# End of a routing stage: scatters one per step, four buffers for places, and the tile table made per partition, ahead of a branch

## The chip, the cores and the metric

The kernel runs on one core of one Trainium2 chip. The metric is the device time of one execution in microseconds (us); below 1% of it, about 22 us, two kernels can hardly be told apart by a few runs, since the runs shown of one kernel differ by as much. PE is TensorE, DVE VectorE, ACT ScalarE, POOL GpSimd and SP SyncE, which here only issues transfers.

## The reference

Two sublayers on 4096 nodes of width 512, with 8 attention heads of 64, 8 experts of 512 hidden units, and 2 experts chosen per node:

```python
x = x + gnn(layernorm(x), adj)          # attention over the neighbours in adj
x = x + moe(layernorm(x))

def moe(xf):
    logits = xf @ Wg + bg                        # 8 experts
    topk_scores, topk_idx = top_k(logits, 2)
    topk_w = softmax(topk_scores)
    h = gelu(einsum('nd,edh->neh', xf, W1) + b1)
    y = einsum('neh,ehf->nef', h, W2) + b2
    sel = take_along_axis(y, topk_idx[:, :, None], axis=1)
    return sum(topk_w[:, :, None] * sel, axis=1)
```

The adjacency matrix is sparse: the attention works on lists of neighbours. In the second sublayer only the two chosen experts of each node are worked out, on tiles of rows that belong to one expert.

## The kernel before

There are three stages.

1. **Projections and lists**: keys, values and queries of all nodes go to DRAM, and lists of neighbours are made.
2. **Attention**: 32 tiles of 128 nodes. For each tile a loop runs over items, one for the diagonal and one for each 128 listed neighbours (L1177 and following). An item's keys, values and mask are fetched nine items ahead (AHEAD = 9) by `fetch`, mostly with indirect transfers issued by POOL. The order of all instructions in this loop is written out by hand (`manual_schedule`), with a step per item.
3. **Feed-forward** (`work_off`): 69 tiles (MOSTLY = NB - 2, NB = 71), each with 128 rows of one expert, read from a DRAM buffer `xs_d` that is ordered by expert.

Between 2 and 3 lies **routing**. When an attention tile is done, its rest runs in the steps after it, as numbered pieces (`piece`), and a group of tiles (four at a time, and for the last tiles 2, 1 and 1) is then routed by a list of `jobs`, one per step in which no other piece uses PE. `route_1` ranks the experts of each node and adds to `count`, the number of nodes per expert and partition. `route_2` and `route_3` find each node's two places in `xs_d` (`slot_i`, whole numbers, L808 and L809) and its two weights. `route_4` issues one scatter on POOL: 128 rows of 2064 bytes to their places. Scatters wait in the list `waiting`. `fetch` issues one in every third step (L263). In the last nine steps nothing is fetched, and the scatters that are left go out either when piece 6 of a later group finds them (then with `at_once`, which lets each wait for the one before to have landed), or in the loop that ends the stage:

```python
while waiting and waiting[0][0] < g - 1:
    waiting.pop(0)[1](True)
```

After the last step, SP loads W2 (eight transfers of 1 MB, L1215) into room that the attention's tiles leave. Then a test of the softmax sums (`bad`, `least`, `redo`, L1227 to L1237) decides whether a slow exact path has to be run: every engine loads `redo` into a register (L1241) and branches (`tc.If(again > 0)`, L1244). With the given inputs the exact path is skipped. In the skipped path each engine brings the semaphores to where the other path would leave them, and SP waits there for its transfers.

Only then comes `finish_routing` (L836 to L893): one product with a matrix of ones sums `count` over the partitions (`pn`). DVE works out, for all 71 tiles of the feed-forward side by side in the free dimension, in every partition alike, which expert a tile belongs to and at which row of `xs_d` it begins. Operations that compare tiles with experts have 71 x 8 = 568 elements per partition. The results are `table` (experts and first rows as whole numbers in one partition), `first` (each partition's row in each tile), `mine` (whether the row belongs to this tile) and `beyond` (whether a 70th and 71st tile exist).

In `work_off`, `fetch(b)` has SP load the tile's first row and expert from `table` into registers (L1372, L1368), then issue the read of 128 rows (L1377) and of two biases (L1379, L1380). PE transposes the rows (`transposed`, L209), multiplies by W1 (L1391), transposes again (L1403), multiplies by W2 (L1420), and POOL adds the weighted rows to the output (L1434).

Outside the attention loop the order of instructions on an engine is a scheduler's, from their order in the program and their dependencies. Inside an engine they are worked off in that order.

Of the kernel before, what the change touches and what calls it, by code (L numbers as in the profile page):

```python
# [43 lines left out]
def kernel(  # L44
# [747 lines left out]
    def route_3(m, l, rank, pp, rows, pool, name):  # L792
# [15 lines left out]
        slot_i = pool.tile([P, m, 2], I32, tag="slot_i", name=f"slot_i_{name}")  # L808
# [27 lines left out]
    def finish_routing(pool, psum):  # L836

        pn = psum.tile([P, E], F32, name="pn")
        nc.tensor.matmul(pn, ones, count, start=True, stop=True)
        many = pool.tile([P, E], F32, name="many")  # L840
        nc.vector.tensor_copy(many, pn)
        more = pool.tile([P, E, NT], F32, name="more")
        nc.vector.tensor_tensor(
            more, many.unsqueeze(2).to_broadcast([P, E, NT]),
            full.unsqueeze(1).to_broadcast([P, E, NT]), op=ALU.is_gt,
        )
        tiles_e = pool.tile([P, E], F32, name="tiles_e")
        nc.vector.tensor_reduce(tiles_e, more, axis=AX.X, op=ALU.add)
        none = pool.tile([P, E], F32, name="none")
        nc.vector.memset(none, 0.0)  # L850
        upto = pool.tile([P, E], F32, name="upto_e")
        nc.vector.tensor_tensor_scan(
            upto, tiles_e, none, initial=0.0, op0=ALU.add, op1=ALU.add
        )
        nc.vector.tensor_scalar(
            none[:1, :1], upto[:1, E - 1 : E], -float(MOSTLY), 0.0, op0=ALU.add, op1=ALU.max
        )
        nc.vector.tensor_copy(beyond, none[:1, :1])
        past = pool.tile([P, NB, E], F32, name="past_e")
        nc.vector.tensor_tensor(  # L860
            past, nth.unsqueeze(2).to_broadcast([P, NB, E]),
            upto.unsqueeze(1).to_broadcast([P, NB, E]), op=ALU.is_ge,
        )

        end = pool.tile([P, E + 1], F32, name="end")
        nc.vector.memset(end[:, E:], float(E * R + P))
        nc.vector.tensor_add(end[:, :E], many, start_e)
        more_e = pool.tile([P, E], F32, name="more_e")
        nc.vector.tensor_sub(more_e, end[:, 1:], end[:, :E])
        ends = pool.tile([P, NB, E], F32, name="ends")  # L870
        nc.vector.tensor_mul(ends, past, more_e.unsqueeze(1).to_broadcast([P, NB, E]))  # L871
        till = pool.tile([P, NB], F32, name="till")
        nc.vector.tensor_reduce(till, ends, axis=AX.X, op=ALU.add)
        expert = pool.tile([P, NB], F32, name="expert")
        nc.vector.tensor_reduce(expert, past, axis=AX.X, op=ALU.add)
        nc.vector.tensor_mul(past, past, tiles_e.unsqueeze(1).to_broadcast([P, NB, E]))  # L876
        nc.vector.tensor_reduce(first, past, axis=AX.X, op=ALU.add)  # L877
        nc.vector.tensor_sub(first, nth, first)
        nc.vector.tensor_scalar(first, first, float(P), float(P), op0=ALU.mult, op1=ALU.add)
        nc.vector.scalar_tensor_tensor(  # L880
            first, expert, float(R), first, op0=ALU.mult, op1=ALU.add
        )
        nc.vector.tensor_scalar_min(first, first, float(E * R))
        nc.vector.tensor_scalar_min(expert, expert, float(E - 1))

        nc.vector.tensor_scalar(till, till, end[:, 0:1], -float(P), op0=ALU.add, op1=ALU.add)
        begin = pool.tile([P, NB], F32, name="begin")
        nc.vector.tensor_tensor(begin, first, till, op=ALU.min)
        nc.vector.tensor_copy(table[:, :NB], expert[:1])
        nc.vector.tensor_copy(table[:, NB:], begin[:1])  # L890
        nc.vector.tensor_add(begin, begin, number.to_broadcast([P, NB]))
        nc.vector.tensor_tensor(mine, begin, first, op=ALU.is_ge)
        nc.vector.tensor_copy(first, begin)  # L893
# [8 lines left out]
    with tc.tile_pool(name="p2a", bufs=2) as two, tc.tile_pool(  # L902
# [15 lines left out]

        half_q = fixed.tile([P, 2, Q4], F32, name="half_q")
# [257 lines left out]
        for n, (i, c) in enumerate(items):  # L1177
            begin()
            if n + AHEAD < len(items):
                fetch(n + AHEAD)  # L1180
            if c == 2 and i + 1 < NT:
                load_q(i + 1)
# [16 lines left out]
            if c == listed[i] - 1:  # L1199
# [11 lines left out]
        nth = endp.tile([P, NB], F32, name="nth")  # L1211
        nc.gpsimd.iota(nth, pattern=[[1, NB]], base=0, channel_multiplier=0,
                       allow_small_or_imprecise_dtypes=True)
        for e in range(E):
            nc.sync.dma_start(out=w2[:, e], in_=W2[e].rearrange("(c p) f -> p c f", p=P))  # L1215
        order.__exit__(None, None, None)
        n = len(items)
        while n <= len(items) + LAST or jobs or first_of_step:
            begin()
            later(n)  # L1220
            while waiting:
# [3 lines left out]

        bad = small.tile([P, NT, 5], F32, name="bad")
        nc.vector.tensor_single_scalar(bad[:, :, 0], fine[:, :, 0], HIGH, op=ALU.is_lt)  # L1227
        nc.vector.tensor_single_scalar(bad[:, :, 1], fine[:, :, 1], 1.0 / LOW, op=ALU.is_lt)
        nc.vector.tensor_single_scalar(
            bad[:, :, 2:].rearrange("p i k -> p k i"), longer, 0.5, op=ALU.is_lt  # L1230
        )
        least = small.tile([P, 1], F32, name="least")
# [272 lines left out]
```

## Time and profile before

| | |
|---|---|
| time, median of 4 runs | 2244.66 us (2228.38 to 2251.49) |
| profiled execution | 2248.23 us, span 2246.5 us |
| mean granted TensorE clock | 0.964 |
| busy, share of the span | PE 93%, DVE 57%, POOL 45%, ACT 41% |
| feed-forward, first PE instruction | 1696.28 us |
| DMA while W2 is loaded (1655 to 1684 us) | 392 GB/s |

The profile is of one execution. Times in it are microseconds from the span's start, durations of single instructions partly in ns. "A <- B" names what an instruction waited for, and "issue" is time in which no wait was seen. PEclk is the TensorE clock that was granted, as a share of the full one; DMA share is the mean busy share of the 16 DMA engines, which comes out a little over 1 when all are full. A row with a "q" (SPq, DVEq) is of an engine's queue of instructions, where branches, waits and register work stand that don't count as busy.

### The profile page before, as it was taken

How to read it: one execution, taken by the hardware profiler on the slowest of the kernel's cores; microseconds unless marked ns; L12 is line 12 of the kernel's file. 1: busy time of each engine (PE TensorE's matmuls, PEld its weight loads, DVE VectorE, ACT ScalarE, POOL GpSimd, SP SyncE). 2: the span in 40 equal slices, each digit the busy share in tenths (PEclk: the TensorE clock that was granted, in tenths of full speed). 3: DMA queues.
4: the chain of work that ended last, by engine and by line, in shares of the span. 5: the costliest groups of instructions: out<-in, count | busy, mean ns of one | idle time of the engine just before them, and what ended most of it. 6: DMA issues, size and time to landing. Idle time of an engine off the chain costs nothing. (4 is left out here: it accounts for less than half of the span.)

```text
span 2246.5 us, 48528 instructions
## 1 busy us (share of the span) xinstructions
PE 2083.8 (93%) x18748; PEld 1384.3 (62%) x18748; DVE 1288.8 (57%) x2446; ACT 931.7 (41%) x1703; POOL 1020.0 (45%) x1067
## 2 busy tenths in 40 slices
PE   8978999899999999989999999998957999999998
PEld 3434444577778777777777777776743444444444
DVE  5786685376666656756666666665663333333332
ACT  3544444354555445545445454454531222222222
POOL 1044455476665565565565555566631111221121
PEclk9999999899999999999999999998988999999999
DMA  8977997677777677777787877766665666566664
GB/s 330 364 269 280 294 317 232 193 227 212 222 242 228 212 234 235 226 226 230 229 244 232 238 220 225 218 200 207 200 246 124 137 139 133 133 133 136 142 136 85
DMA packets 213087, 479.03 MB, mean 213 GB/s; under 512 B 48962, under 2 KB 80962, under 8 KB 208756
## 3 DMA queue, kind: packets, MB, share of 16 engines
q0 software_dynamic: 78944, 241.65, 36.8%
q1 hardware_dynamic: 133380, 233.15, 34.3%
q8 instruction: 153, 2.51, 0.5%
q10 hardware_dynamic: 528, 1.05, 0.1%
q14 instruction: 82, 0.67, 0.1%
HBM read 398.85 MB, written 76.90 MB: 212 GB/s over the span
## 5 line engine op out<-in xcount | busy, mean ns | idle before, releaser
L231 POOL DMA_INDIRECT kv<-kv_d,key_of x363 | 404.9, 1115 | 399.8 <-PE po L1024 239.7
L1012 DVE TENSOR_TENSOR e<-e,mask 128x512 f32<-128x512 f32 (+1 forms) x363 | 322.5, 889 | 304.8 <-ACT e L1004 148.2
L957 ACT COPY kT<-pk 128x512 f32<-128x512 f32 x395 | 232.3, 588 | 368.8 <-PE pk L954 215.6
L1024 PE MATMUL po<-e,kv 128*64 128x64 f32 (+1 forms) x5808 | 323.5, 250 | 16.7 <-issue 16.4
L1030 DVE TENSOR_TENSOR acc<-acc,e 128x512 f32<-128x512 f32 (+1 forms) x363 | 321.1, 885 | 2.8 <-PE po L1024 1.7
L1434 POOL DMA_INDIRECT out_dram<-y,to x69 | 107.7, 1561 | 453.0 <-ACT y L1426 442.0
L231 POOL DMA_INDIRECT mask<-in_adjT_dram,mask_of x234 | 277.8, 1187 | 72.8 <-issue 63.4
L1024 PEld LDWEIGHTS po<-e,kv 128*64 128x64 f32 x5808 | 252.3, 139 | 68.7 <-issue 24.6
L1001 PE MATMUL s<-q,kT 128*128 128x128 f32 x1832 | 281.2, 299 | 0.2
L1391 PE MATMUL ph<-w,xT 128*128 x552 | 251.7, 599 | 1.0 <-ACT xT L210 1.0
L1420 PE MATMUL py<-w,hT 128*128 x552 | 248.6, 593 | 1.5 <-DVE hT L1405 1.5
L1001 PEld LDWEIGHTS s<-q,kT 128*128 128x128 f32 x1832 | 236.0, 201 | 17.4 <-issue 1.2
L954 PE MATMUL pk<-ident,kv 64*128 64x64 f32 x2904 | 178.2, 241 | 49.8 <-issue 28.3
L954 PEld LDWEIGHTS pk<-ident,kv 64*128 64x128 f32 x2904 | 124.7, 143 | 121.3 <-issue 82.2
L1004 ACT ACTIVATE e<-s 128x512 f32<-128x512 f32 x229 | 137.7, 601 | 94.9 <-PE s L1001 54.3
L994 ACT ACTIVATE e<-s 128x512 f32<-128x512 f32 x268 | 147.3, 597 | 65.7 <-PE po L1024 26.2
L989 PE MATMUL s<-q,kT 64*128 64x128 f32 x2144 | 161.2, 282 | 3.6 <-issue 2.5
L1391 PEld LDWEIGHTS ph<-w,xT 128*128 128x128 f32 x552 | 100.5, 192 | 101.8 <-issue 100.2
L1420 PEld LDWEIGHTS py<-w,hT 128*128 128x128 f32 x552 | 99.6, 190 | 102.2 <-issue 99.5
L231 POOL DMA_INDIRECT pm<-in_adjT_dram,mask_of x129 | 126.1, 977 | 74.8 <-issue 30.8
L1426 ACT ACTIVATE y<-y,gate 128x512 f32<-128x512 f32 x69 | 49.8, 722 | 256.9 <-DVE y L1425 252.5
L1429 DVE SCALAR_TENSOR_TENSOR to<-r,spare,mine 128x1 f32<-128x1 int32 x69 | 15.2, 220 | 232.5 <-DMA r<-xs_d 232.5
(611 smaller groups left out, 2742.8 us busy)
## 6 DMA issues: line engine op xcount, KB each, us to landing
adjT<-in_adjT_dram SPq DMA_DIRECT2D x32, 2048.0 KB
bb<-in_L_ffn_b_dram SPq DMA_DIRECT2D x138, 256.0 KB
r<-xs_d SPq DMA_DIRECT2D x69, 258.0 KB
kv_d<-kv SPq DMA_DIRECT2D x32, 512.0 KB
xt<-in_x_dram SPq DMA_DIRECT2D x32, 256.0 KB
qT_d<-qT SPq DMA_DIRECT2D x8, 1024.0 KB
q<-qT_d SPq DMA_DIRECT2D x64, 128.0 KB
xr<-in_x_dram SPq DMA_DIRECT2D x32, 256.0 KB
```

What stands on the lines that cost most here:

```text
L231: nc.gpsimd.indirect_dma_start(out=to, out_offset=None, in_=src, in_offset=bass.IndirectOffsetOnAxis(ap=of[:, at[i] + c : at[i] + c + 1], ...
L954: nc.tensor.transpose(pk[:, r, ts(p, KD)], kv[n][half, ts(p, P)], ident[half, half])
L957: nc.scalar.copy(kT[n].rearrange("k p (r j) -> k r p j", r=2), pk[:, :, : NP * KD].rearrange("k r (p j) -> k r p j", p=NP),)
L989: nc.tensor.matmul(s[r][:, p, :], k[rows, p, :], q_in[i][rows, p, r, :], start=True, stop=True,)
L994: nc.scalar.activation(e.rearrange("p (a r) q -> p r a q", r=2)[:, r], s[r], AF.Exp)
L1001: nc.tensor.matmul(s[:, p], k[:, p, :], q_in[i][:, p, :, q], start=True, stop=True)
L1004: nc.scalar.activation(e, s.rearrange("p a r q -> p (a r) q"), AF.Exp)
L1012: nc.vector.tensor_mul(e, e, m.unsqueeze(1).to_broadcast(e.shape))
L1024: nc.tensor.matmul(po[i][r * KD : (r + 1) * KD, p, q], v[:, ts(h, KD)], e[:, h, :], start=(c < 0 and p == 0), stop=(c == listed[i] - 1), s ...
L1030: nc.vector.tensor_add(acc[i][:, :, q], acc[i][:, :, q], e)
L1391: nc.tensor.matmul(ph, xTs[b][:, c, :], w1[:, bass.ds(es[b], 1), c, :], start=(c == 0), stop=(c == DC - 1),)
L1420: nc.tensor.matmul(py, hTs[b][:, c, :], w2[:, bass.ds(es[b], 1), c, :], start=(c == 0), stop=(c == HC - 1),)
```

## The change

Four parts:

- In the last nine steps of the attention loop, where nothing is fetched, each step issues one scatter if any waits, behind a memset of one column on POOL.
- `slot_i` has four buffers instead of the pool's two.
- The test of the softmax sums is put among the last steps of routing (`check_all` at the fourth step after the last item) instead of behind them.
- `finish_routing` is called ahead of the branch, and once more inside it, at the end of the exact path. It works out one tile per partition: tile number = partition number, experts in the free dimension (8 elements per operation), then spreads expert, first row and a third column over all partitions by a diagonal matrix of 3 x 71 columns and a product with a matrix of ones. The number of tiles of an expert comes from a shift instead of a comparison with 32 multiples.

```diff
-        slot_i = pool.tile([P, m, 2], I32, tag="slot_i", name=f"slot_i_{name}")
+        slot_i = pool.tile([P, m, 2], I32, tag="slot_i", bufs=4, name=f"slot_i_{name}")
...
-    def finish_routing(pool, psum):
+    def finish_routing(all_ones, pool, psum, tag, name):
+        def column(what, width=1):
+            return pool.tile([P, width], F32, name=f"{what}_{name}")
+        pn = psum.tile([P, E], F32, tag=tag, name=f"pn_{name}")
         nc.tensor.matmul(pn, ones, count, start=True, stop=True)
+        tiles_i = pool.tile([P, E], I32, name=f"tiles_i_{name}")
+        nc.vector.tensor_scalar_add(tiles_i, pn, float(P - 1))
+        nc.vector.tensor_single_scalar(
+            tiles_i, tiles_i, P.bit_length() - 1, op=ALU.arith_shift_right
+        )
+        tiles_e = column("tiles_e", E)
+        nc.vector.tensor_copy(tiles_e, tiles_i)
...
+        past = column("past_e", E)
+        nc.vector.tensor_scalar(past, upto, number, None, op0=ALU.is_le)
+        both = pool.tile([P, 2, E], F32, name=f"both_{name}")
+        nc.vector.tensor_mul(both[:, 0], past, more_e)
+        nc.vector.tensor_mul(both[:, 1], past, tiles_e)
+        of = column("of", 3)
+        nc.vector.tensor_reduce(of[:, 0:1], past, axis=AX.X, op=ALU.add)
+        sums = column("sums", 2)
+        nc.vector.tensor_reduce(sums, both, axis=AX.X, op=ALU.add)
+        own = of[:, 2:3]
...
+        nc.vector.tensor_tensor(of[:, 1:2], own, till, op=ALU.min)
+        diag = pool.tile([P, 3, NB], F32, name=f"diag_{name}")
+        nc.vector.tensor_mul(
+            diag, ident[:, :NB].unsqueeze(1).to_broadcast([P, 3, NB]),
+            of.unsqueeze(2).to_broadcast([P, 3, NB]),
+        )
+        pt = psum.tile([P, 3, NB], F32, tag=tag, name=f"pt_{name}")
+        nc.tensor.matmul(pt, all_ones, diag, start=True, stop=True)
+        nc.vector.tensor_copy(table.rearrange("p (k b) -> p k b", k=2), pt[:1, :2])
+        nc.vector.tensor_scalar(first, pt[:, 1], number, None, op0=ALU.add)
+        nc.vector.tensor_tensor(mine, first, pt[:, 2], op=ALU.is_ge)
...
+        between = fixed.tile([P, 1], F32, name="between")
...
             if n + AHEAD < len(items):
                 fetch(n + AHEAD)
+            elif waiting:
+                nc.gpsimd.memset(between, 0.0)
+                waiting.pop(0)[1]()
...
-        nth = endp.tile([P, NB], F32, name="nth")
-        nc.gpsimd.iota(nth, pattern=[[1, NB]], base=0, channel_multiplier=0,
-                       allow_small_or_imprecise_dtypes=True)
+        all_ones = endp.tile([P, P], F32, name="all_ones")
+        nc.gpsimd.memset(all_ones, 1.0)
...
         while n <= len(items) + LAST or jobs or first_of_step:
             begin()
             later(n)
+            if n == len(items) + 4:
+                check_all()
             while waiting:
                 waiting.pop(0)[1]()
             n += 1
-        bad = small.tile([P, NT, 5], F32, name="bad")
...
+        finish_routing(all_ones, endp, ps_e, "e", "")
...
             scatters[:] = first_scatters
-    with tc.tile_pool(name="ps_end", bufs=1, space=PSUM) as psum:
-        finish_routing(endp, psum)
+        with tc.tile_pool(name="g4", bufs=1) as one, tc.tile_pool(
+            name="g4p", bufs=1, space=PSUM
+        ) as psum:
+            finish_routing(all_ones, one, psum, "n", "g")
```

`check_all` holds the lines of the old test unchanged.

## The prediction

> **What bounds the kernel now.** I read the busy times by stretch first, to find the stage that the change touches.
>
> ```profile
> core 0: us, PE busy (x) PEld busy (x) DVE busy (x) ACT busy (x) POOL busy (x), PEclk, DMA share, GB/s
> 1655.00:1684.00 29.00, 8.46 (x49) 4.52 (x48) 13.20 (x85) 3.02 (x8) 10.00 (x11) 0.64 1.03 392
> 1684.00:1693.00 9.00, 0.17 (x1) 0.10 (x1) 7.63 (x26) 0.00 (x0) 0.00 (x0) 0.50 0.03 11
> 1693.00:1697.00 4.00, 0.72 (x4) 0.72 (x4) 0.49 (x4) 0.00 (x0) 0.00 (x0) 0.50 0.58 130
> ...
> 1705.00:2200.00 495.00, 494.21 (x1533) 243.54 (x1532) 173.63 (x448) 119.14 (x194) 98.35 (x63) 1.00 0.63 136
> ```
>
> From 1705 us on PE is full (494.21 of 495 us): the feed-forward stage costs the same whenever it starts, so the change is worth what it moves that start. Ahead of it lie two different stretches. From 1655 to 1684 the DMA engines are full at 392 GB/s: eight loads of W2 (1 MB each, issued from 1652.4 on) and the last scatters. From 1684 to 1693 the DMA is empty and only DVE works. That is the table, alone on the path. The chain of waits says the same:
>
> ```profile
> 1684.51 0.18 PE pn L839
> ...
> 1691.66 0.09 DVE table L889
> 1691.76 0.14 DVE table L890
> ...
> 1693.00 0.37 SPq L1377
> ...
> 1693.91 3.54 DMA bb<-in_L_ffn_b_dram
> 1697.45 0.60 ACT xT L210
> ```
>
> The read of the first tile's rows is issued 1.1 us after the table's last value (1691.9 to 1693.0), and PE's first transpose stands at 1696.28 in the timeline, so table's end to PE is 4.4 us. Now what stands ahead of the table: the instructions of the branch (L1244) on each queue, and two waits.
>
> ```profile
> L1244 SPq EVENT_SEMAPHORE  x8: 17/17/17, 1681.3 to 1684.9; - x8
> L1244 SPq COMPARE_BRANCH  x1: 50/50/50, 1675.8 to 1675.8; - x1
> L1244 PEldq COMPARE_BRANCH  x1: 6184/6184/6184, 1675.9 to 1675.9; - x1
> ...
> L1244 DVEq COMPARE_BRANCH  x1: 72/72/72, 1678.7 to 1678.7; - x1
> ...
> L1244 DVEq EVENT_SEMAPHORE  x1: 21/21/21, 1684.3 to 1684.3; - x1
> ```
>
> ```profile
> PE pn L839 <- DVEq L1244: 9.7, 1, 9.7
> ...
> DVE slot_i L809 <- DMA xs_d<-rows,slot_i: 8.3, 2, 6.3
> ```
>
> DVE reaches the branch at 1678.7 and does its first act behind it at 1684.3, 5.6 us later (SP 5.5 us, PE 6.2 us). SP's eight semaphore instructions there last until 1684.9: in the skipped path SP waits for its own loads, W2 with them. So three things end within a microsecond of each other: DVE behind the branch (1684.3), W2 landed (1684.9) and the DMA idle (1684). Only after them does the table start. The second row says that DVE twice waited for scatters to land before it might overwrite places (slot_i), 8.3 us in all.
>
> **The change part by part.**
>
> *Table ahead of the branch.* Removed from the path: everything from pn (1684.51) to the last table value (1691.9), 7.4 us, of which five operations of 128x568 at 0.73 to 0.75 us are 3.7. What SP waits for next is its own last semaphore at 1684.9, since DVE's is at 1684.3. If both stay where they are, SP's first table load moves from 1691.9 to 1684.9, and everything behind it by the same 7.0 us.
>
> *Does DVE get behind the branch as early as before, with the table in front of it?* The order of the changed program puts about 35 DVE instructions behind the last count: 24 of the table, 11 left of the last group's places and weights. Before, that count stood at 1674.43, held up by the 6.3 us stall for places. With four buffers the stall goes (no buffer is shared with a group whose scatters are under way). The logits come at 1669.2 (PE L749, 1668.57 plus 0.59) and not at 1672.58, 3.4 us earlier; but in the new order the last tile's statistics stand some five small operations (0.1 us each) further back, which I take as 0.6. So the count comes 2.8 us earlier, at 1671.6. From it: 35 operations at 0.15 us (128x8 and 128x1 rows last 0.14 to 0.17) are 5.3; a wait for ACT's exponential 0.3; diag of 128x213, between 0.23 (128x71) and 0.42 (128x256), 0.4; PE's product with 213 columns 0.6 (a 512-column product takes 0.85 at the half clock, so 0.36, and 0.2 from PE to DVE); three reads of it 0.6. End: 1678.8; with 0.5 to the branch 1679.3, against 1678.7 before. With 5.6 behind the branch DVE is at 1684.9, level with SP. I take 1684.9 for both.
>
> Bounds. From above: two scatters of 258 KB leave the full stretch (below), at 392 GB/s 1.3 us, so W2 lands at 1683.6; with DVE as early, the gain is 8.3. From below: every one of the 35 operations at 0.25 us puts DVE at the branch at 1682.8, and 5.6 behind it at 1688.4: gain 3.5. If ACT's 0.2 us through the same branch (1676.0 to 1676.2) held for DVE, SP's 1684.9 would decide again.
>
> *Scatters.* In the old kernel the eight scatters of the last full group go out from 1632.74 to 1665.14, the later ones each behind the landing of the one before (2.1 to 6 us idle). Now six go one per step, each behind a memset of 128x1 on POOL; the nearest row, an iota of 128x71, is 0.23 us, so with 0.3 us between, six cost at most 3.2 us of POOL, in a stretch where POOL idles over 15 us. The seventh and eighth still wait for a landing, but by about 1652 rather than 1658 and 1665, ahead of W2. Nobody waits for POOL there. If that cover were gone, 3.2 us would be late on the scatters of the next group, which wait for DVE at 1661.5 in any case.
>
> *Last scatters.* Their places now come near 1673, their weights near 1675, so the last is issued at about 1676 rather than 1680.30. In the full stretch a scatter landed 7.0 us after its issue (1670.42, DVE released at 1677.46): 1683. That is before 1684.9, so the first read does not wait for it.
>
> DVE's copies beside scatters deserve a weighing: the scatters beside a busy DVE took 1.47 to 2.55 us (1632 to 1645), those beside an idle one 0.97. The Trainium skill (SBUF — State Buffer, "SBUF: two separate sides") has it that a DMA issued by GpSimd cannot write its descriptors while DVE copies in a two-port mode, with about 620 ns going to 3100 ns. By that page the last two would lose some 2.1 us each, an estimate, land by 1687.2 and leave a gain of 4.7. By the rows alone they lose up to 1.6 us each and land by 1686.2, which would cut the gain to 5.7. The operations beside those slow scatters last 0.7 to 1.2 us, the table's 0.15, so I put nothing in the sum.
>
> *Costed at nothing.* The test of the softmax sums moves earlier: redo comes at 1660 and not 1674.86, but SP's 1684.9 hides that (without that cover SP would gain, not lose); its product stands ahead of PE's L782, 0.17 us, while DVE is busy. The memset of ones replaces the iota of 0.23 us. The copy of the table inside the branch is not executed. A new 4-byte tile moves others by 32 to 96 bytes; operations of 128x512 cost the same on tiles apart (L1012 889 ns, L1030 885), so nothing. PE stays at half clock (0.50 until 1704) since it idles over 10 us in either kernel: the eight first products take 6.68 us instead of 3.44 as now.
>
> *Sum.* The profiled execution took 2248.23 us (span 2246.5, 1.7 around it). Minus 7.0 is 2241.2. That execution lies 3.6 above the median of the runs shown, 2244.66; minus 7.0, that is 2237.7, 0.3% less.
>
> **Rivals.**
>
> *Cover lost by code.* SP waits 7.0 us (1684.9 to 1691.9) and PE 11.6 us for the table and rows; new code can load there unseen. If SP needs a block of code behind the join at the price that the branch shows (5.5), the gain is 1.5: 2243.2. If PE then needs one as well (6.2), after the rows have landed, it is 4.7 us slower: 2249.4. It decides from 7.0 us uncovered. For it: the 5.5 to 6.2 us rows. Against: those fell in the full DMA, which is idle behind 1684.9, and SP's instructions behind 1691.9 run without a gap.
>
> *DVE late.* The table's chain becomes the wait that replaces the table: gain 3.5, 2241.2. For it: the level finish (1684.9 for both). Against: 0.15 us rows.
>
> *More than the table.* If what holds DVE and SP behind the branch is the DMA queue and not the bytes, an earlier branch could open all by 1681.3, SP's first semaphore: gain 10.6, 2234.1. Against: SP waits for W2, whose bytes fill the DMA until 1684.
>
> *It does nothing:* the table is hidden anyway. The idle DMA and the chain speak against it: 2244.7.
>
> **How the numbers follow.** Main case 0.68 (2236.4 to 2241.2 by the bounds), DVE late 0.12, code 0.10 (half of it slower than before), more 0.06, nothing 0.04. A measurement of this kernel tells about 1%, 22 us, from no change, and the runs shown differ by 23 us; no case reaches 22 us, so faster or slower by over 1% comes from that spread and from what I have not seen: 0.10 and 0.06, within 1% 0.84. The range adds about 10 us of spread of a median to the cases: 2226 to 2249.
>
> **What would show it.** Right: no wait of slot_i for scatters; pn ahead of the branch near 1672; SP's first table load within a microsecond of its last L1244 semaphore, near 1685; first transpose near 1689; the same 550 us behind it. Wrong: SP's table load waiting for DVE after 1687, a hole on SP or PE behind the join, or an attention stage that ends elsewhere than 1659.

## The result, and the profile after

The changed kernel takes 2240.27 us (median of 52 runs, 2227.1 to 2254.01). The kernel before, run beside it, takes 2245.74 us (78 runs, 2228.38 to 2255.98). The ratio of the runs is 0.998 with a 95% interval of 0.997 to 0.999: the change saves about 4.5 us, with 2.2 to 6.7 as its interval; the medians differ by 5.5 us. The profiled execution of the changed kernel took 2237.78 us (span 2236.1) against 2248.23 (span 2246.5), 10.4 us less span. That is more than the runs say, and the first thing to settle is how much of it is the change.

The stretches of the profile after, in the same view as before (busy time by engine, granted clock, DMA share):

```profile
core 0: us, PE busy (x) PEld busy (x) DVE busy (x) ACT busy (x) POOL busy (x), PEclk, DMA share, GB/s
1651.00:1680.00 29.00, 9.98 (x53) 5.29 (x52) 15.38 (x110) 3.02 (x8) 7.79 (x8) 0.63 0.98 365
1680.00:1682.00 2.00, 0.00 (x0) 0.00 (x0) 0.00 (x0) 0.00 (x0) 0.00 (x0) 0.50 0.03 8
1682.00:1686.00 4.00, 0.75 (x4) 0.71 (x4) 0.49 (x4) 0.00 (x0) 0.00 (x0) 0.50 0.49 121
1686.00:1700.00 14.00, 11.74 (x30) 5.21 (x28) 2.03 (x10) 3.56 (x5) 0.00 (x0) 0.76 0.98 190
1700.00:2200.00 500.00, 499.62 (x1548) 246.53 (x1549) 173.88 (x452) 118.64 (x193) 99.76 (x64) 1.00 0.62 136
```

The 9 us in which only DVE worked, with the DMA empty, have shrunk to 2 us in which nobody works (1680 to 1682). What follows is as before: four transposes at the half clock, 14 us in which the DMA is full again (0.98) though it moves only 190 GB/s, and then a full PE.

The branch, now line 1262:

```profile
L1262 SPq EVENT_SEMAPHORE  x8: 17/17/17, 1673.9 to 1681.0; - x8
L1262 SPq COMPARE_BRANCH  x1: 50/50/50, 1667.8 to 1667.8; - x1
...
L1262 PEldq COMPARE_BRANCH  x1: 6264/6264/6264, 1672.4 to 1672.4; - x1
L1262 DVEq COMPARE_BRANCH  x1: 72/72/72, 1674.4 to 1674.4; - x1
...
L1262 DVEq EVENT_SEMAPHORE  x1: 21/21/21, 1680.0 to 1680.0; - x1
```

DVE reaches the branch at 1674.4, has the table done by then, and is behind it at 1680.0. SP's last semaphore there stands at 1681.0, and its first load of rows follows at once. The chain of waits (start, duration, what), which had the table's operations in it before:

```profile
1681.04 0.28 SPq L1391
...
1682.12 0.37 SPq L1396
...
1690.43 8.86 DMA r<-xs_d
1699.31 0.23 DVE to L1448
...
1699.65 0.69 DVE hT L1424
...
1700.38 3.70 PE py L1439 x8
```

No table, and no wait for it, is left in the chain. A new link is: the first product with W2 (py, 1700.38) comes from DVE's copy hT, and DVE, which works in order, stood at a small operation on the *fourth* tile's rows (to, L1448) until these landed at 1699.31. The profile's list of DVE's waits has no row of slot_i for scatters any more.

To compare kernels whose attention stage ends at different times, all milestones below are counted from the issue of the first load of W2: 1652.39 us in the profile before (L1215) and 1648.62 in that after (L1228).

```profile
1648.62 1.87 SPq L1228 DMA_DIRECT2D w<-in_L_ffn_W_dram  x3
```

So "DVE at the branch" is 1674.4 - 1648.62 = 25.8. "First rows" is the first PE transpose of the feed-forward stage (pt_e), "first py" the first product with W2.

| us after the first load of W2 | before | after |
|---|---|---|
| DVE at the branch | 26.3 | 25.8 |
| DVE behind the branch | 32.0 | 31.4 |
| SP's last semaphore at the branch | 32.5 | 32.4 |
| table ready | 39.5 | 24.5 |
| first load of rows issued | 40.6 | 33.5 |
| first rows transposed | 43.9 | 36.6 |
| first py | 57.8 | 51.8 |
| first py to the end of the span | 536.4 | 535.7 |

The 10.4 us fall apart into 3.8 that lie ahead of the first load of W2 (1652.39 less 1648.62), 6.0 up to the first py, and 0.7 behind it (a rounding of 0.1 beside). So behind that load 6.7 us are gained. But the load is no fixed point: the scatters in the last steps lie ahead of it. Counted from the third last tile's product with Wo (py, L1071 before and L1081 after), which lies ahead of all these steps, the load comes 39.0 us later in the kernel before and 41.0 in the changed one. PE's rows of that stretch, before and after:

```profile
1613.37 3.70 PE L1071 MATMUL py<-wo,o 128*128 128x512 f32 x8
...
1635.46 1.16 PE L1062 MATMUL rb<-rinv,spread 128*128 128x128 f32 x8
...
1638.92 0.46 PE L954 MATMUL pk<-ident,kv 64*128 64x64 f32 x8
```

```profile
1607.58 3.70 PE L1081 MATMUL py<-wo,o 128*128 128x512 f32 x8
...
1629.68 1.16 PE L1072 MATMUL rb<-rinv,spread 128*128 128x128 f32 x8
...
1632.20 0.58 PE L999 MATMUL s<-q,kT 64*128 64x128 f32 x5 [0.23 <-issue]
...
1635.13 0.46 PE L964 MATMUL pk<-ident,kv 64*128 64x64 f32 x8
```

Here rb and pk are products of the attention loop. From rb to this pk PE takes 3.46 us before and 5.45 after, while POOL sends a scatter per step: that is all of the 2.0. Of the traces of the experiments below, those with the steps on the chip whose runs last about 2258 us show the same (6.30 us in e12, 6.25 in e11), those without them do not (3.46 in e9 and e10). On the chips at 2101 and 2104 us it is 3.45 with the steps (e7) and 3.46 without (e4). What holds PE there no run shows.

From that product to the end of the span the kernel before takes 633.1 us and the changed one 628.5. So the pair of executions gains 4.6 us, and the runs say 4.5 (2.2 to 6.7); one pair can agree so closely by chance. The other 5.8 of the 10.4 (1613.37 less 1607.58) are an attention stage that ran earlier in this execution; as the runs spread over 27 us, I count them as no part of the change.

### The profile page after: what moved, and what is told of

Read it like the earlier page. It is cut to its first block, busy times and chain, and to the rows that moved or that the text cites. A ratio compares the mean times of both kernels' runs of the same rounds, so it can differ in the third digit from the quotient of the medians.

```text
span 2236.1 us, 48530 instructions
## 1 busy us (share of the span) xinstructions
PE 2076.3 (93%) x18750; PEld 1376.4 (62%) x18750; DVE 1281.2 (57%) x2444; ACT 930.0 (42%) x1703; POOL 1021.1 (46%) x1073
## 5 line engine op out<-in xcount | busy, mean ns | idle before, releaser
L1034 PE MATMUL po<-e,kv 128*64 128x64 f32 (+1 forms) x5808 | 323.4, 249 | 21.3 <-issue 20.3
L1034 PEld LDWEIGHTS po<-e,kv 128*64 128x64 f32 x5808 | 251.8, 138 | 74.0 <-issue 29.9
L1011 PE MATMUL s<-q,kT 128*128 128x128 f32 x1832 | 275.4, 294 | 0.8 <-issue 0.6
L1011 PEld LDWEIGHTS s<-q,kT 128*128 128x128 f32 x1832 | 230.4, 197 | 18.1 <-issue 2.3
L1410 PEld LDWEIGHTS ph<-w,xT 128*128 128x128 f32 x552 | 100.5, 192 | 101.3 <-issue 100.2
L1448 DVE SCALAR_TENSOR_TENSOR to<-r,spare,mine 128x1 f32<-128x1 int32 x69 | 15.1, 220 | 239.3 <-DMA r<-xs_d 239.3
```

Source lines behind the costliest of these rows:

```text
L1011: nc.tensor.matmul(s[:, p], k[:, p, :], q_in[i][:, p, :, q], start=True, stop=True)
L1034: nc.tensor.matmul(po[i][r * KD : (r + 1) * KD, p, q], v[:, ts(h, KD)], e[:, h, :], start=(c < 0 and p == 0), stop=(c == listed[i] - 1), s ...
L1410: nc.tensor.matmul(ph, xTs[b][:, c, :], w1[:, bass.ds(es[b], 1), c, :], start=(c == 0), stop=(c == DC - 1),)
```

## The experiments

Theory A was that of the prediction: the place of the table, ahead of the branch, makes the gain, by taking the table off the path behind SP's last semaphore. Theory B was that the four buffers for places and the scatters in the steps make it, since DVE then comes to the branch earlier. The runs brought two more: theory D, that the order in which rows and biases are loaded is the next limit, and theory E, that SP's wait for W2 and its neighbours is a floor that several parts of the change reach without each other.

The experiments ran on other chips than the result, in three groups with the kernel before at 2101.37, 2104.2 and 2258.27 us, so ratios and milestones can be compared, and times only within a group. The kernel before has a trace on the result's chip alone; the changed kernel's milestones repeat on the third group's chip within 0.8 us (e12). In the third group the runs of one kernel spread by about 1%, and times there tell little.

| kernel | median us (before, same chip) | ratio, 95% | DVE at branch | SP's last | table ready | first load of rows | first rows | first py |
|---|---|---|---|---|---|---|---|---|
| e1_behind | 2096.18 (2101.37) | 0.9976, 0.9964 to 0.9989 | 21.3 | 33.3 | 31.9 | 34.5 | 37.5 | 52.4 |
| e2_wide_ahead | 2094.28 (2101.37) | 0.9968, 0.9958 to 0.9978 | 28.1 | 31.6 | 26.9 | 33.3 | 36.6 | 51.4 |
| e3_two_places | 2095.62 (2101.37) | 0.9974, 0.9964 to 0.9983 | 26.0 | 32.2 | 24.9 | 33.3 | 36.5 | 50.3 |
| e4_no_steps | 2094.62 (2101.37) | 0.9967, 0.9955 to 0.9979 | 26.9 | 34.2 | 26.0 | 35.4 | 38.7 | 52.5 |
| e5_no_branch | 2098.11 (2104.2) | 0.9974, 0.9963 to 0.9985 | none | none | 23.8 | 31.6 | 34.6 | 48.3 |
| e6_w2_late | 2099.22 (2104.2) | 0.9983, 0.9971 to 0.9994 | 25.3 | 29.4 | 24.2 | 31.1 | 34.5 | 55.0 |
| e7_rows_first | 2093.79 (2104.2) | 0.9951, 0.9938 to 0.9965 | 25.3 | 32.6 | 24.4 | 33.7 | 36.8 | 50.5 |
| e8_rows_first_w2_late | 2099.57 (2104.2) | 0.9979, 0.9969 to 0.9990 | 25.6 | 29.1 | 24.4 | 31.4 | 34.7 | 55.2 |
| e9_four_places | 2259.92 (2258.27) | 0.9996, 0.9973 to 1.0019 | 20.7 | 34.5 | 34.1 | 35.6 | 38.8 | 54.4 |
| e10_table_alone | 2256.06 (2258.27) | 0.9986, 0.9963 to 1.0009 | 29.9 | 32.6 | 28.9 | 35.1 | 38.3 | 52.1 |
| e11_rows_first_warm | 2263.18 (2258.27) | 1.0029, 1.0009 to 1.0049 | 25.2 | 31.8 | 24.2 | 33.0 | 36.6 | 46.8 |
| e12_changed_again | 2258.69 (2258.27) | 1.0005, 0.9985 to 1.0024 | 25.8 | 32.7 | 24.7 | 33.8 | 36.9 | 51.0 |

### The place alone: e1_behind

```
-        finish_routing(all_ones, endp, ps_e, "e", "")
...
-            finish_routing(all_ones, one, psum, "n", "g")
+    with tc.tile_pool(name="ps_end", bufs=1, space=PSUM) as psum:
+        finish_routing(all_ones, endp, psum, "n", "")
```

The new form of the table is called once, behind the branch.

> The changed kernel, but with the per-partition table called once, behind the branch, where the old one stood. Measure: time from the issue of the first W2 load to PE's first transposed rows; 43.9 us in the old kernel, 36.6 in the changed one. Theory A (the gain is the table's place: the table is off the path, and what ends last is W2's landing at SP): the new table comes back on the path with its own length, about 4.5 us from its first product to its last table value, so about 41, and the kernel is 4 to 5 us slower than the changed one, 2 to 3 us faster than the old. Rival B (the gain is in the places and scatters, which end earlier): 36.6 and the time of the changed kernel.

It is as fast as its neighbours, 0.9976 (0.9964 to 0.9989). The branch in its trace, and the table's last steps on DVE:

```profile
L1261 SPq EVENT_SEMAPHORE  x8: 17/17/17, 1530.8 to 1538.7; - x8
...
L1261 DVEq COMPARE_BRANCH  x1: 72/72/72, 1526.7 to 1526.7; - x1
...
L1261 DVEq EVENT_SEMAPHORE  x1: 21/21/21, 1532.6 to 1532.6; - x1
```

```profile
1537.08 0.29 DVE L896 CAST table<-pt__21337 1x142 int32<-1x142 f32 x1 [1.23 <-PE pt__21337 L895]
```

Without the table ahead of it DVE comes to the branch at 21.3 instead of 25.8, is behind it at 27.1 (1532.6 less 1505.44), and has the table at 1537.37, ahead of SP's last semaphore at 1538.7. First rows come at 37.5, not at the 41 of theory A. The table is hidden behind the branch as well as ahead of it. Theory A fell: the place is one way to the gain, not the only one.

### The form of the table: e2_wide_ahead

The old formula, with its six operations of 128x568, stands ahead of the branch in place of the new one.

```
+    def finish_routing(nth, pool, psum, tag, suffix):
...
+        past = pool.tile([P, NB, E], F32, name=f"past_e{suffix}")
+        nc.vector.tensor_tensor(
+            past, nth.unsqueeze(2).to_broadcast([P, NB, E]),
+            upto.unsqueeze(1).to_broadcast([P, NB, E]), op=ALU.is_ge,
+        )
```

> The changed kernel, but with the old wide formula of the table (71 tiles x 8 experts per operation) ahead of the branch. Its DVE work from the last count to the branch is about 4 us longer than the new form's (9.3 against 5.4 us). Theory A, with DVE 5.6 us behind the branch whatever the DMA does: DVE comes behind the branch 2.9 us after SP's last wait, so first rows at 39.5 us after the first W2 load, 3 us slower than the changed kernel. Theory A, with that 5.6 us shorter once the DMA is idle: 36.6 to 38. Rival C (the gain is in the form, not in the place): 41 or more.

It loses nothing: 0.9968 (0.9958 to 0.9978), first rows at 36.6 as in the changed kernel. DVE comes to the branch 2.3 us later (28.1), but is behind it after 4.1 us (1534.7 to 1538.8, the branch being L1254 there) rather than 5.6, at 32.2, 0.6 behind SP's last semaphore. The first load of rows follows DVE there, by 1.1 us. With the place, the narrow form is worth nothing that these runs show.

### The places and the steps: e3_two_places, e4_no_steps

```
-        slot_i = pool.tile([P, m, 2], I32, tag="slot_i", bufs=4, name=f"slot_i_{name}")
+        slot_i = pool.tile([P, m, 2], I32, tag="slot_i", name=f"slot_i_{name}")
```

> The changed kernel with two buffers for places, as before. Theory A: the scatters of the last full group land before W2 starts, so the 6.3 us wait doesn't come back; the last group's places wait for the group of two at most 0.5 us; first rows at 36.6 to 37.2 us, time equal within 1 us. Rival B: the waits of 8.3 us come back, DVE reaches the branch that much later, first rows at 41 to 45 us.

No loss: 0.9974 (0.9964 to 0.9983), first rows at 36.5. The wait of slot_i for scatters does not come back, though there are two buffers again: the scatters of the last full group now go out in the steps, and their buffer is free in time. So with the steps the four buffers are not needed.

```
-            elif waiting:
-
-                nc.gpsimd.memset(between, 0.0)
-                waiting.pop(0)[1]()
```

> The changed kernel without the scatters in the last nine steps (they go out one behind the landing of the other, as before), with four buffers for places. Theory A: two scatters of 258 KB come back into the stretch in which the DMA is full, 1.3 us at 392 GB/s; first rows at 36.6 to 38, time 0 to 1.3 us more. Rival B: first rows at 40 or more.

No loss in time: 0.9967 (0.9955 to 0.9979). The milestones show one: SP's last semaphore is at 34.2 and first rows at 38.7, 2.1 later than after the whole change. It need not come from the steps: PE's last product of the attention stage begins as early after the first load of W2 as elsewhere, but takes 5.40 us instead of 3.70 in this execution, at a granted clock of 0.58 and 0.50, so it ends 1.6 us later than in the changed kernel (8.85 against 7.2 us). How much of the 2.1 is the steps stays open; the ratio doesn't show it.

### Each part alone: e9_four_places, e10_table_alone

e9 is the kernel before with one edit:

```
-        slot_i = pool.tile([P, m, 2], I32, tag="slot_i", name=f"slot_i_{name}")
+        slot_i = pool.tile([P, m, 2], I32, tag="slot_i", bufs=4, name=f"slot_i_{name}")
```

> The old kernel with four buffers for places as its only edit. Theory E (the gain is a floor that several parts can reach: SP's wait for W2, 32 to 33 us after the first W2 load; what matters is when DVE reaches the branch plus what it still has to do behind it): without the stall DVE reaches the branch at about 21.5 us rather than 26.3, is behind it 5.6 to 5.8 us later, at 27.2, and the wide table of 7.5 us ends at 34.7 rather than 39.5; first rows at 39 (43.9 in the old kernel), time 4 to 5 us less than before. Theory A (place alone): first rows at 43 to 44, no gain.

```profile
L1244 SPq EVENT_SEMAPHORE  x8: 17/17/17, 1692.9 to 1702.2; - x8
...
L1244 DVEq COMPARE_BRANCH  x1: 72/72/72, 1688.4 to 1688.4; - x1
...
L1244 DVEq EVENT_SEMAPHORE  x1: 21/21/21, 1694.2 to 1694.2; - x1
```

```profile
1701.61 0.18 DVE L890 CAST table<-begin 1x71 int32<-1x71 f32 x1
```

Without the stall for places DVE reaches the branch at 20.7 instead of 26.3. The old table, wide operations and all, behind the branch, is done at 1701.8, just ahead of SP's last semaphore at 1702.2. First rows come at 38.8: one word of the diff brings 5.1 of the 7.3 us (43.9 to 36.6) that the whole change brings. The time does not show it (0.9996, 0.9973 to 1.0019), but the interval, from 6 us faster to 4 slower, could hide it. The steps alone and the earlier test alone were not run on the kernel before.

e10 is the changed kernel with the edits of e3 and e4 together, so the table alone is left of the change.

> The changed kernel without the scatters in the last steps and with two buffers for places: the table in its new form ahead of the branch, with the stalls of the old kernel. Theory E: the last count comes at 22 us after the first W2 load as in the old kernel, DVE reaches the branch at 27.5 to 28.5 and is behind it at 32 to 34, about level with SP's wait for W2; first rows at 36.5 to 38, so the table alone brings 6 to 7 of the 7.3 us, as four places, steps and form bring most of them without it. Rival B (places and scatters decide): first rows at 41 or more.

```profile
L1258 SPq EVENT_SEMAPHORE  x8: 17/17/17, 1695.2 to 1703.2; - x8
...
L1258 DVEq COMPARE_BRANCH  x1: 72/72/72, 1700.5 to 1700.5; - x1
...
L1258 DVEq EVENT_SEMAPHORE  x1: 21/21/21, 1704.5 to 1704.5; - x1
```

The stall of 5.8 us for places is back, DVE comes to the branch at 29.9, and is behind it at 33.9, after SP. That is the rival "DVE late" of the prediction, shown on the chip. First rows come at 38.3: the table alone brings 5.6 of the 7.3 us. So the parts aren't additive, 5.1 and 5.6 against 7.3 together. Each lets the table end ahead of the floor, and whichever does it first leaves little to the other. This is theory E, and e1, e2, e9 and e10 agree with it. The floor is not one number: SP's last semaphore lies between 31.6 (e2) and 34.5 (e9) where all eight loads of W2 go out early. And it is not SP's alone. In every trace with the branch and the table ahead of it, the first load of rows follows the later of two things by 1.1 us: SP's last semaphore, or DVE behind the branch. It is DVE in e2 (32.2), e6 (30.0), e8 (30.2) and e10 (33.9), and SP in the others.

All these milestones begin at the first load of W2, so what the steps cost ahead of it on this chip is not in them. From the third last tile's product with Wo to the end of the span e10, without the steps, takes 626.7 us, e9 629.1 and e12, the whole change, 631.3. These are single traces, and the intervals of the runs don't tell the three apart; whether the table without the steps is the better change on such a chip stays open.

### What the floor is: e5_no_branch, e6_w2_late

e5 leaves out the branch with the exact path in it, which this input does not take. The cut is long; its first lines:

```
-    again = nc.values_load(
-        redo, min_val=0, max_val=P, skip_runtime_bounds_check_because="counts partitions"
-    )
-    with tc.If(again > 0):
...
```

> The changed kernel without the branch and the exact path inside it (left out: the path for inputs that fail the test of the softmax sums). Nothing jumps, and SP no longer waits for W2 before it reads the table. Theory A (what ends last in the changed kernel is the join of the branch: SP's wait for W2 and DVE's 5.6 us): the first read of rows is issued about 1.1 us after the table's value, some 25 us after the first W2 load; the rows queue with W2 for the DMA and land 5 to 7 us later, so first rows at 30 to 33 us rather than 36.6. The pace of the stage stays bound by W2 and by the rows and biases of four tiles, which all go through the full DMA, so the first product with W2 comes 1 to 4 us earlier than 51.8. Rival (the rows wait for the DMA, not the branch): 36 to 37, and no gain.

The first load of rows comes only 1.9 us earlier (31.6 against 33.5), though the table is ready at 23.8. SP's waits say what it stands for (line, releaser, us in total, times, longest):

```profile
SPq L1281 <- DMA xs_d<-rows,slot_i: 4.2, 2, 3.0
...
SPq L1281 <- DMA out_dram<-xr: 2.6, 1, 2.6
```

SP waits for the last scatters to have landed and for its own last store of the attention stage, 6.8 us in all, while W2 fills the DMA. So the floor is the full DMA more than the branch; the branch is some 2 us of it. First rows come at 34.6, between the 30 to 33 that were expected and the rival's 36 to 37; the first py comes at 48.3, 3.5 earlier than in the changed kernel, and the ratio does not show it.

e6 thins that DMA out: the last three of the eight loads of W2 are issued behind the loads of the first four tiles.

```
+        load_w2(0, EARLY)   # EARLY = 5
...
+            if from_b == 0:
+                load_w2(EARLY, E)
```

> The changed kernel with five of the eight W2 loads where they were and three (3 MB) issued behind the reads of the first four feed-forward tiles. Theory A: SP's last semaphore behind the branch no longer waits for 3 MB, 8 us at 392 GB/s, so DVE behind the branch decides: if its 5.6 us are due to a full DMA they shrink and first rows come at 29 to 32 us, if not at 35 to 36. The three loads then land behind rows and biases, so the first product with W2 comes at 50 to 54 us (51.8 in the changed kernel), about even in time. If first rows stay at 36.6, W2's landing isn't what SP waits for.

The floor moves: SP's last semaphore is at 29.4, and DVE, behind the branch at 30.0, is now what the first load of rows follows; first rows come at 34.5. But the first py comes at 55.0, 3.2 us later than in the changed kernel, since the late loads of W2 now land last. Two of PE's waits:

```profile
PE py L1443 <- DMA w<-in_L_ffn_W_dram: 2.9, 1, 2.9
...
PE py L1443 <- DVE hT L1428: 0.9, 1, 0.9
```

The bytes are the same, so what the rows gained W2 lost. By the ratio, 0.9983 (0.9971 to 0.9994), it is no better than its neighbours.

### The next limit: e7_rows_first, e8_rows_first_w2_late, e11_rows_first_warm

In the changed kernel the rows of tiles 2 to 4 are issued each behind two loads of biases. e7 sends them ahead (one bias of the first tile excepted):

```
+            loads = {}
             for b in range(from_b, min(from_b + 4, to_b)):
-                fetch(b)
+                loads[b] = fetch(b, parts=True)
+                loads[b][0]()
+                if b == from_b:
+                    loads[b][1](0)
+            for b in loads:
+                if b > from_b:
+                    loads[b][1](0)
+                loads[b][1](1)
```

> The changed kernel, but at the start of the feed-forward stage the rows of the first four tiles are read ahead of their biases (only the first tile's first bias comes behind its rows). Theory D (why 7.3 us at the first rows are only 6.0 us at the first product with W2, and 5.5 in the medians): DVE's queue is in order, and the small operation on the fourth tile's rows stands ahead of the copy of the first hidden tile; so the fourth tile's rows, 17.2 us after the first, set the start of the pace. With rows first they land within 8 us, and the first product with W2 comes 4 to 6 us earlier (46 to 48 us after the first W2 load instead of 51.8); the kernel is 3 to 6 us faster than the changed one. Rival (the pace waits for PE's half clock and ACT's table load, not for rows): no change.

The wait for the fourth tile's rows is gone; DVE has them 3.9 us after the first transpose (1545.43 less 1541.54) rather than 14.1 (1699.31 less 1685.25). But the first py comes at 50.5, where 46 to 48 was expected. That is 1.3 earlier than in the changed kernel's first trace, and no earlier than in e3 (50.3), which has the old order and in which PE does not wait for that copy at all. So the old order costs PE between nothing (e3, e5) and 1.5 us (e9) there, by the execution. DVE, PE and ACT in turn show what took its place:

```profile
1545.43 0.22 DVE L1460 SCALAR_TENSOR_TENSOR to<-r,spare,mine 128x1 f32<-128x1 int32 x1 [0.25 <-DMA r<-xs_d]
```

```profile
1543.34 6.54 PE L1422 MATMUL ph<-w,xT 128*128 x8 [0.72 <-ACT xT L210]
```

```profile
1550.96 1.28 ACT L1428 ACT_TABLE_LOAD   x1
```

The first eight products run at half clock (6.54 us), and ACT loads its table (1.28 us) ahead of the first gelu. By ratio e7 is the fastest kernel of the study, 0.9951 (0.9938 to 0.9965). It beats the kernel before. Whether it beats the changed kernel isn't settled: its milestones gain 1.3 us, the changed kernel wasn't in its group, and its interval touches that of e3 (0.9964 to 0.9983), the nearest relative of the changed kernel in another.

e8 has the edits of e6 and e7 together.

> Both: rows first, and three W2 loads behind the first four tiles' rows and biases. If first rows move as theory A has it (29 to 36 us after the first W2 load), the first product with W2 waits for the late loads: 44 to 50 us; 3 to 8 us faster than the changed kernel. If the late loads land later than that, it is slower than with rows first alone.

First py at 55.2, where 44 to 50 was expected: the late W2 is again what ends last, and rows ahead of biases do not help then. 0.9979 (0.9969 to 0.9990).

e11 takes away the two limits that e7 left. It adds, behind the branch, work whose results nobody uses:

```
+    nc.scalar.activation(warm, first[:, :1], AF.Gelu)
...
+        for k in range(4):
+            nc.tensor.matmul(pw, first, w1[:, 0, k, :], start=True, stop=True)
```

> The changed kernel with rows first (as in the earlier run), and behind the branch four products on PE whose result isn't used, and a one-column gelu on ACT whose result isn't used. Theory F (with rows first, the start of the feed-forward stage is set by PE at half clock, 6.5 us for the first eight products instead of 3.4, and by ACT's table load of 1.28 us ahead of the first gelu): the first product with W2 comes 3 to 4.5 us earlier than with rows first alone (50.5 us after the first W2 load), at 46 to 47.5, and the kernel is 2.5 to 4.5 us faster than that one, 5 to 8 faster than the changed one. Rival (biases or rows come late again): 49 or more, no gain.

PE and DVE in its trace:

```profile
1712.19 3.70 PE L1428 MATMUL ph<-w,xT 128*128 x8 [0.72 <-ACT xT L210]
...
1720.98 3.60 PE L1457 MATMUL py<-w,hT 128*128 x8
1729.54 1.11 PE L1440 MATMUL pht<-ident,h 128*128 128x128 f32 x4 [4.96 <-ACT h L1434]
```

```profile
1727.79 0.22 DVE L1466 SCALAR_TENSOR_TENSOR to<-r,spare,mine 128x1 f32<-128x1 int32 x1 [8.50 <-DMA r<-xs_d]
1728.05 0.16 DVE L1470 TENSOR_TENSOR to<-to,spare 128x1 int32<-128x1 f32 x1
1728.13 0.69 DVE L1433 TENSOR_TENSOR h<-ph,bb 128x512 f32<-128x512 f32 x1
```

The first eight products take 3.70 us, and the first py comes at 46.8 (1720.98 less 1674.23), 4.2 earlier than in e12, the changed kernel on that chip. Then DVE stands 8.50 us at the *fifth* tile's rows, which are queued behind seven loads of biases, PE stands 5 us, and all is given back: the span ends 589.1 us after the first load of W2, against 589.4 in e12. The runs are even slower than those of the kernel before, 1.0029 (1.0009 to 1.0049), 2 to 11 us; nothing in this stretch shows why. The DMA carries the same rows and biases in any order. Most of its time goes to the biases, as the last section shows. What is shown is that each limit taken away brings out the next within 5 us; that the loads' bytes are the last of them is only argued.

### The changed kernel once more: e12_changed_again

No edit.

> The changed kernel itself, on the chip of the other three. Ratio to the old kernel 0.997 to 0.999 as measured; first rows at 36 to 37.5 us after the first W2 load, first product with W2 at 50 to 52.5.

The milestones repeat: DVE at the branch 25.8, first rows 36.9 (36.6 in the first profile), first py 51.0 (51.8). The time does not show the gain on this chip: 1.0005 (0.9985 to 1.0024), that is from 3.4 us faster to 5.4 slower. From the first py to the end its span takes 538.5 us, 2.8 more than the first profile. The result's 2.2 to 6.7 us and this interval overlap; neither excludes that the gain differs from chip to chip.

## Why the prediction was right, and where not

*The sum was right but for its size.* 2237.7 was said and 2240.27 came. The stated range, 2226 to 2249, also holds 2244.7, the forecast's case that nothing changes, so the time alone confirms little; the milestones do that. The kernel before stands at 2245.74 by 78 runs, 1.1 above the median of four that the sum was made against; the other 1.5 is the gain, 5.5 by medians instead of 7.0. By the ratio it is 4.5, and 7.0 lies just outside its 2.2 to 6.7.

*SP's last semaphore decides:* right. It was said to stay where it is, and it went from 32.5 to 32.4. The first load of rows follows it by 1.1 us and moved by 7.1, first rows by 7.3.

*The count 2.8 us earlier:* right, 2.7 (1667.98 in the profile after, 19.4 after the first load of W2, against 22.0).

*The chain on DVE from the count to the branch:* too long. 7.7 us with the last 0.5 were said, and it takes 6.4 (1667.98 to 1674.4). Operations of the table and of the last group are issued in turn, as these rows of DVE show, 0.07 to 0.09 us from one start to the next, while each lasts 0.15:

```profile
1668.34 0.16 DVE L804 TENSOR_REDUCE top<-part 128x2 f32<-128x16 f32 x1
1668.41 0.16 DVE L845 TENSOR_SCALAR tiles_i__19799<-pn__19797 128x8 int32<-128x8 f32 x1
1668.48 0.17 DVE L806 TENSOR_TENSOR is_k<-is_k,place 128x16 f32<-128x16 f32 x1
1668.57 0.15 DVE L812 TENSOR_TENSOR less<-top 128x1 f32<-128x1 f32 x1
```

Two chains that don't wait for each other overlap; the sum priced them one after the other. Another term was too small: from the end of diag (1671.62) to the first read of PE's product (1672.86) are 1.24 us, and 0.6 were said. In all DVE came 0.5 us ahead of where it was before, not 0.6 behind, and was not level with SP but 1.0 ahead (1680.0 against 1681.0). The error lay on the safe side of SP's wait and cost the sum nothing.

*The 5.6 us behind the branch:* right, 1674.4 to 1680.0.

*"Everything behind it by the same 7.0":* this is one of two terms that were mis-sized. First rows moved by 7.3, the first py by 6.0. In both kernels the copy hT ahead of the first py stands in DVE's order behind the fourth tile's rows. These landed 56.7 us after the first load of W2 before (1709.08) and 50.7 after (1699.31), 6.0 earlier: the fourth load was issued 8.3 us after the first (1690.43 less 1682.12) instead of 7.8, and took 8.86 us to land instead of 8.26. Before, PE was busy until just then and did not wait; after, it waits 1.4 us. In e7, with the rows first, the wait is gone. It differs with the execution as well: against the one trace before, the first py moved by 6.8 in e12, where PE waits 0.4 us, and by 7.5 in e3, where it does not wait. A stall that I had read as the whole path's (PE's half clock) had a second one right beside it. Behind the first py 0.7 came back, in one pair of executions.

*Scatters:* right on POOL. The seventh and eighth go out at 1640.21 and 1644.68, ahead of W2, the eighth after a wait of 2.61 us for a landing; the memsets last 0.11 us. The last of all is issued at 1671.88, 23.3 after the first load of W2, where 23.6 was said, and first rows do not wait for it. But the steps were put at nothing, and this is the second mis-sized term: in this trace PE loses 2.0 us in them (3.46 against 5.45 from rb to pk), which brings the 6.7 behind the load of W2 down to 4.6 (a rounding of 0.1 beside). The forecast's own sign against itself, an attention stage that ends elsewhere than 1659, came too: the last product with Wo ended at 1655.8 and not at 1659.7. The third last tile's product, ahead of the steps, was already 5.8 us earlier, so the steps are not what brought that; they took 2.0 of it back.

*The weighing:* neither price was paid. The last two scatters on POOL, beside the table's operations on DVE:

```profile
1670.61 0.97 POOL L825 DMA_INDIRECT xs_d<-rows,slot_i  x1 [4.82 <-DVE till__19827 L884]
1671.88 0.97 POOL L825 DMA_INDIRECT xs_d<-rows,slot_i  x1 [0.31 <-DVE diag__19830 L890]
```

Both last 0.97 us, as beside an idle DVE. Of the old scatters from 1632 to 1645 that were read as 1.47 to 2.55 us, one, at 1636.28, took 0.99, so even beside long operations of DVE the loss was not in every one. The Trainium skill (SBUF — State Buffer, "SBUF: two separate sides") says that GpSimd cannot write a transfer's descriptors while DVE runs an operation in a two-port mode. No such loss shows here; whether any of the operations beside them runs in that mode, no run shows.

*Two readings* were off without touching the sum. Six operations of 128x568, not five, stood in the old table, 4.4 us of the 7.4. And the 889 and 885 ns are means over operations of 128x512 and 128x1024.

*The rivals.* Code behind the join did not show: SP goes from its last semaphore to the first load in 1.1 us. "More than the table" did not happen in the changed kernel, and e5 and e6 show why: opening earlier is worth 1.9 to 2.4 us at the first load of rows, and in e6 W2's bytes take it back. "DVE late" is what e10 became, and e2 by 0.6 us.

*The reason behind the sum was too narrow.* It gave the gain to the table's place. e1 and e9 show that the table where it was, but shorter or started earlier, ends ahead of the floor as well.

## What to carry to other kernels

Before a chain of work is moved or shortened, find the wait that ends next behind it, and ask which parts of the change reach that floor alone: here four buffers for a 128x2 tile, one word, reach within 2.2 us of the whole change at the first rows. Behind a floor made by a full DMA, reordering loads moves the wait from one consumer to another (W2, the fourth tile's rows, the fifth's), so follow the order of landing through all of the first tiles before promising a gain. And count a gain from a point ahead of every part of the change: from the first load of W2 the 2 us that PE loses in the steps are out of sight. On an in-order engine, a tiny operation on late data holds up everything behind it; look for it ahead of every copy that PE needs.

## What the hardware showed that I had not expected

DVE's time through the branch isn't a constant. It is 5.6 to 5.9 us when the branch is reached 21 to 27 us after the first load of W2 with all of W2 under way (the DMA share in that time is 0.97 before, 0.79 after, 1.04 in e1 and e9), and 4.0 to 4.1 when it is reached at 28 to 30 (share 0.38 in e2, 0.43 in e10); in e6, with less in the DMA (0.52), 4.7. ACT needs 0.2 us at the same branch. The profile's DMA queues for instructions carry nothing from 1660 to 1667 in the profile after, and 8 packets from 1667 to 1681, where SP, PE and DVE stand behind the branch. That looks like code that is loaded through a busy DMA. No run moved the code, so the cause is argued, not shown. The Trainium skill (Runtime: NRT & Kernel Launch, "Instruction fetch mechanics") says that a taken branch out of the part of the code that is at hand has to wait for a DMA fetch.

The DMA can be full at half its rate. From 1686 to 1700 its share is 0.98 at 190 GB/s, while W2 and the scatters moved 365 GB/s at the same share. The loads there are rows, and biases that one row of DRAM feeds to 128 partitions: a packet takes 152 ns on the mean there (98.2% of 16 engines' 14 us over 1450 packets), against 84 for those of SP's queue from 1656 to 1668, nearly all of W2 (80.4% of 16 engines' 12 us over 1833). The trace of e7, where the rows go ahead, shows that the biases are the slow ones: from 1542.6 to 1545, nearly all rows, 361 GB/s at 100.2% of 16 engines, and from 1546 to 1549.5, biases alone, 135 GB/s at 105.2%. At that rate the eight biases of the first four tiles, 256 KB each, take some 15.5 us, an estimate, and the four tiles' rows some 2.9.
